# Group norm on one Trainium2 core: scale and offset of the packed blocks from a matrix product, and the inverse root's first guess read from PSUM

## The chip, the cores and the metric

The kernel runs on one core of one Trainium2 chip. The metric is the device time of one execution in microseconds (us), taken as the median of several executions. Beside these timed runs there is one profiled execution, whose hardware profile (the page and the trace) gives the durations, starts and waits of every instruction. Where the text gives a time such as "at 1079.81", it is counted from the start of that execution's span.

A core has five engines with queues of their own: PE (TensorE, matrix products; PEld is its loading of weights), DVE (VectorE), ACT (ScalarE), POOL (GpSimd) and SP (SyncE, which issues most DMAs here). SBUF is the on-chip memory of 128 partitions ("rows"), PSUM the small memory into which PE writes.

## What is computed

The input x has shape (16, 56, 56, 384): 16 images, 384 channels last, float32. Two residual layers follow each other, each of which works on a group norm (32 groups of 12 channels, statistics over a whole image):

```python
def _gn(v, G=32, eps=1e-5):
    g = v.reshape(B_, H_, W_, G, C_ // G)
    m = jnp.mean(g, axis=(1, 2, 4), keepdims=True)
    s = jnp.var(g, axis=(1, 2, 4), keepdims=True)
    return ((g - m) / jnp.sqrt(s + eps)).reshape(v.shape)
...
x = x + _L0_conv_ref(_gn(x), L0_conv_w_qkv, L0_conv_w_proj, L0_conv_b_proj)
x = x + _L1_conv_ref(_gn(x), L1_conv_w)
```

Layer 0 (`_L0_conv_ref`) is a dilated neighbourhood attention: a 384 to 1152 product gives q, k and v, 12 heads of 32 channels attend to 3x3 neighbours with dilation 1, 2 or 3 (four heads each), and a 384 to 384 product projects the result. Layer 1 (`_L1_conv_ref`) is a depthwise 3x3 convolution whose taps are the signs of `w`.

## The kernel before, in words

**Tiling.** An image is cut into 7 chunks of 8 image rows (PX = 448 pixels), so there are 112 chunks m = 7b + c. Work is done with channels on the partitions: three blocks of 128 channels (NG = 3).

**Stages of a chunk.** `plan_a` loads x, transposes it to channels-first (PE, pt_x, L478), takes statistics (`bn_stats`, L493) and stores it in DRAM (xd). `plan_b` loads it again, normalises it on ACT, makes q, k, v (products pq and pkv, L530, copied out by ACT: k at L543), multiplies q and k (DVE, t, L595), sums by head (PE, ps, L576), takes the softmax (transposes pt_s, L619), spreads the weights over the channels (PE, pb_a, L663), multiplies them with v (DVE, w, L674), sums over neighbours (POOL, L684, L687, L688) and projects (po, L701). `plan_c` does the convolution ten chunks later. Two of its three channel blocks use **packed blocks**: a tile z holds, for 4 sets q of 32 channels, the three vertical neighbours ky on 3 x 32 = 96 partitions, so that one product (pc, L825) does a column of taps. `normalise` (L792, on ACT; for the last set of the last image L788, on DVE) applies scale and offset to z and takes them from mrz, which must lie on the 96 partitions in z's layout. `column` (L815, ACT) starts pc from the middle taps with scalars that `column_scalars` (L727 to L737, POOL) makes. The third block is done by ACT's products m (L897) and POOL's sums (L907, L912, L915). Results are transposed back (PE, pt_o, L924), copied by ACT (osb, L930) and stored (out_dram, L933).

**Group norm** (`group_norm`, L349 to L419) runs 18 times. Each normal call holds two sets (L = 2): layer 1 of image b, and layer 0 of image b + 2; four calls hold only one. Sixteen of them include a layer 1 set (`for_convolution`). Its steps, each a piece between two `yield`s:

- DVE: `bn_aggr`, mean and variance of each channel over the chunks (ch).
- PE pm (L363): sums over the 12 channels of a group, three products with the selector gsel (128 rows x 32 columns); DVE L365 scales it into pair.
- PE pb (L370): the group's mean back on the channels with gselT (32 rows x 128 columns); DVE dev L373, POOL L375, L376: squared deviation plus channel variance.
- PE pv (L381): group sums of that. DVE L385 makes the variance plus eps (v); L388 and L389 make a first guess of 1/sqrt(v) by integer arithmetic on v's bits (shift right by one, then constant minus it).
- POOL L392 to L395, three times: Newton steps; L396: the offset. pair then holds offset and scale for 32 groups on 32 partitions.
- PE pp (L401): offset and scale on the channels; DVE L404 copies them to mr.
- SP: mr goes to DRAM as mrd (L409), and in the next piece three DMAs (L414) read it back in z's layout as mrz.

pm, pb, pv, pp, pt_x, pkv, po, pt_s and pt_o all take turns in two PSUM buffers (ps_mt).

**Order of the work.** Every piece has a due time, written out by hand in the table WHEN and counted in units of which a chunk has STEP = 9; a group norm of layer 1 of image b begins at STEP x (7b + 6) plus the offsets of WHEN["statistics"]. All pieces are sorted by time and issued in that order. Between FROM = 81 and UNTIL = 1022 units each engine's queue is pinned to the order in which pieces are issued (`pin`, for PE, DVE, ACT, POOL and SP). Before and after that, so in the first nine chunks of work and in the convolutions of the last image, a scheduler of the tile framework chooses the order by its own reckoning. At the start selectors are built by POOL from memsets and affine selections, in parallel with the weight loads. In the last image no attention stands beside the convolution any more, z is called z_last and xg is called xg_last there, and the third block's taps are done by DVE (`taps_last`, L888).

Of the kernel before, what the change touches and what calls it, by code (L numbers as in the profile page):

```python
# [8 lines left out]
F32 = mybir.dt.float32  # L9
BF16 = mybir.dt.bfloat16  # L10
I32 = mybir.dt.int32
AF = mybir.ActivationFunctionType
ALU = mybir.AluOpType
# [4 lines left out]
P = 128  # L18
HEADS = 4
HD = 32  # L20
NG = 3
NTAP = 9
NQ = 4
# [3 lines left out]
GN_CH = 12  # L27
GN_G = 32
# [3 lines left out]
RSQRT_BITS = 0x5F3759DF  # L32
# [9 lines left out]
    v=[[11.109, 11.185, 12.149], [14.632, 15.913, 18.706], [17.166, 18.74, 20.057]],  # L42
# [29 lines left out]
def dilated_attention_then_binary_conv(  # L72
# [28 lines left out]
    nc = tc.nc  # L101
    B, H, W, C = x.shape
    PX = ROWS * W
# [5 lines left out]
    K3 = 3 * HD  # L109
    JG = NG - 1  # L110

    def place(p):

        g, o = divmod(p, NTAP)
        return NG * o + g
# [4 lines left out]
    const = ctx.enter_context(tc.tile_pool(name="const", bufs=1))  # L120
    ps_mt = ctx.enter_context(tc.tile_pool(name="ps_mt", bufs=2, space=PSUM))
# [19 lines left out]
    for p in range(NPAD):  # L141

        v = place(p) if p < NG * NTAP else p
        nc.gpsimd.affine_select(
            out=perm[:, v, :], in_=perm[:, v, :], compare_op=ALU.not_equal, fill=1.0,
            base=-(32 * (p % 4) + 4 * (p // 4)), pattern=[[-1, HEADS]], channel_multiplier=1,
# [1 line left out]
    permf = perm.rearrange("p v h -> p (v h)")  # L148


    gsel = const.tile([P, NG, GN_G], F32, name="gsel")
    gselT = const.tile([GN_G, NG, P], F32, name="gselT")
    nc.gpsimd.memset(gsel, 1.0)
    nc.gpsimd.memset(gselT, 1.0)
    for j in range(NG):
        for lo, s in ((0, 1), (GN_CH - 1, -1)):
            nc.gpsimd.affine_select(
                out=gsel[:, j], in_=gsel[:, j], compare_op=ALU.is_ge, fill=0.0,
                base=s * P * j + lo, pattern=[[-s * GN_CH, GN_G]], channel_multiplier=s,
            )  # L160
            nc.gpsimd.affine_select(
                out=gselT[:, j], in_=gselT[:, j], compare_op=ALU.is_ge, fill=0.0,
                base=s * P * j + lo, pattern=[[s, P]], channel_multiplier=-s * GN_CH,
            )


    wqkvT = const.tile([P, NG, 3 * C], F32, name="wqkvT")
# [16 lines left out]
    st_p = ctx.enter_context(tc.tile_pool(name="st_p", bufs=2))  # L184
    dr_p = ctx.enter_context(tc.tile_pool(name="dr_p", bufs=3, space=DRAM))
# [4 lines left out]
    y_p = ctx.enter_context(tc.tile_pool(name="y_p", bufs=4))  # L190
# [3 lines left out]
    xg_p = ctx.enter_context(tc.tile_pool(name="xg_p", bufs=2))  # L194
    m_p = ctx.enter_context(tc.tile_pool(name="m_p", bufs=3))
    o_p = ctx.enter_context(tc.tile_pool(name="o_p", bufs=2))


    kv = []
# [149 lines left out]
    def group_norm(sets):  # L349

        L = len(sets)
        ch = st_p.tile([P, L, NG, 2], F32, tag=f"ch{L}", name="ch")
# [4 lines left out]
                        nc.vector.bn_aggr(ch[:, n, j, :], stats()[:, j].rearrange("p c s -> p (c s)"))  # L357
            yield

        pair = st_p.tile([GN_G, L, 3], F32, tag=f"pair{L}", name="pair")  # L360
        pm = ps_mt.tile([P, 512], F32, tag="mt", name="pm")
        for j in range(NG):
            nc.tensor.matmul(pm[:GN_G, 0:L], gsel[:, j], ch[:, :, j, 0], start=(j == 0), stop=(j == NG - 1))  # L363
        yield
        nc.vector.tensor_scalar_mul(pair[:, :, 2], pm[:GN_G, 0:L], -1.0 / GN_CH)  # L365
        yield

        pb = ps_mt.tile([P, 512], F32, tag="mt", name="pb")
# [3 lines left out]
        dev = st_p.tile([P, L, NG], F32, tag=f"dev{L}", name="dev")  # L372
# [5 lines left out]

        pv = ps_mt.tile([P, 512], F32, tag="mt", name="pv")
        for j in range(NG):  # L380
            nc.tensor.matmul(pv[:GN_G, 0:L], gsel[:, j], dev[:, :, j], start=(j == 0), stop=(j == NG - 1))  # L381
        yield
        var = st_p.tile([GN_G, 3, L], F32, tag=f"var{L}", name="var")
        v, r, t = var[:, 0], var[:, 1], var[:, 2]
        nc.vector.tensor_scalar(v, pv[:GN_G, 0:L], 1.0 / GN_CH, 1e-5, op0=ALU.mult, op1=ALU.add)  # L385

        ri = r.bitcast(I32)
        nc.vector.tensor_single_scalar(ri, v.bitcast(I32), 1, op=ALU.arith_shift_right)  # L388
        nc.vector.tensor_scalar(ri, ri, -1, RSQRT_BITS, op0=ALU.mult, op1=ALU.add)  # L389
        yield  # L390
        for step in range(3):
            nc.gpsimd.tensor_tensor(t, r, r, ALU.mult)  # L392
# [1 line left out]
            nc.gpsimd.tensor_scalar(t, t, -0.5, 1.5, op0=ALU.mult, op1=ALU.add)  # L394
            nc.gpsimd.tensor_tensor(pair[:, :, 1] if step == 2 else r, r, t, ALU.mult)  # L395
        nc.gpsimd.tensor_tensor(pair[:, :, 0], pair[:, :, 2], pair[:, :, 1], ALU.mult)  # L396
        yield

        pp = ps_mt.tile([P, 512], F32, tag="mt", name="pp")
        for j in range(NG):  # L400
            nc.tensor.matmul(pp[:, 2 * L * j : 2 * L * (j + 1)], gselT[:, j], pair[:, :, 0:2], start=True, stop=True)  # L401
        yield
        mr = st_p.tile([P, NG, L, 2], F32, tag=f"mr{L}", name="mr", bufs=5 - L)
        nc.vector.tensor_copy(mr.rearrange("p j l s -> p (j l s)"), pp[:, : 2 * L * NG])  # L404
        yield
        mrz = None
        if sets[0][2]:
            mrd = dr_p.tile([P, JG, 2], F32, tag="mrd", name="mrd")
            nc.sync.dma_start(mrd, mr[:, :JG, 0, :])  # L409
        yield  # L410
        if sets[0][2]:
            mrz = st_p.tile([K3, JG, NQ, 2], F32, tag="mrz", name="mrz")
            for ky in range(3):
                nc.sync.dma_start(  # L414
                    mrz[ky * HD : (ky + 1) * HD], mrd.rearrange("(q c) j s -> c j q s", c=HD)
                )
        yield
        for n, (_, done, for_convolution) in enumerate(sets):
            done(mr[:, :, n], mrz) if for_convolution else done(mr[:, :, n])  # L419
# [643 lines left out]
```

## Time and profile before

| what | value |
|---|---|
| median of 3 executions | 5050.63 us (5050.13 to 5052.91) |
| profiled execution | 5050.42 us |
| its span on the core | 5048.7 us, so 1.7 us lie around it |
| mean granted PE clock | 0.977 of full speed |
| busy: PE, DVE, POOL, ACT | 96%, 89%, 84%, 51% of the span |
| group norms: pm begins | 46.7, 237.2, then every 299 us or so from 479.2 to 4658, last 4904.3 |
| products of the group norm, records | pm 108, pb 108, pv 108, pp 108 |
| mrd<-mr, mrz<-mrd | 16 and 48 DMAs, 2 KB each, 6.9 and 2.9 us from issue to landing |

A page of the profile gives busy time and share of each engine, a chart in 40 slices, and the chain of work that ended last (followed back from the last instruction, at each step to what released it). Below these stand groups of instructions, `line engine operation out<-in (partitions x elements) xcount | busy, mean ns of one | idle time of the engine before them, and what ended most of it`. The view of one tile adds `min/median/max` in ns. In a timeline a line is `start us, length us, engine, line, operation`, with the engine's idle time before it in brackets. Float32 products appear as two records of weights and matmul each, so three products of the code are "x6".

### The profile page before, as it was taken

To read this page: it belongs to the slowest core of one execution; us is meant where nothing else is said; L and a number is where in the kernel's file an instruction comes from. 1 tells how busy PE (TensorE), PEld (TensorE's weight loads), DVE (VectorE), ACT (ScalarE), POOL (GpSimd) and SP (SyncE) were. 2 spreads that over 40 slices of the span, in tenths; PEclk is the share of its full clock that TensorE was granted. 3 is DMA by queue.
4 is the path that set the end of the run, shared out by engine and by line. 5 is a ranking of instruction groups with operands and counts; after the bars stand their busy time and mean duration, and the time that the engine had idled before them with its cause. 6 is when DMAs were issued, how large, how long until landed. Compare 5 with 4: busy or idle time off the path is not lost.

```text
span 5048.7 us, 69318 instructions
## 1 busy us (share of the span) xinstructions
PE 4833.2 (96%) x23433; PEld 2213.7 (44%) x23433; DVE 4513.4 (89%) x4710; ACT 2573.4 (51%) x4645; POOL 4226.0 (84%) x2894
## 2 busy tenths in 40 slices
PE   7999999999999999999999999999999999999954
PEld 4444444444444444444444444444444444444421
DVE  4888999999999999999999999999999999999846
ACT  3212555555555555555555555555555555555454
POOL 2677889988888888888889888888888888999970
PEclk9999999999999999999999999999999999999965
DMA  5434666666666666666666666666666666655554
GB/s 172 122 100 123 179 175 171 175 172 177 174 177 178 170 176 167 179 177 173 174 168 174 178 177 178 175 176 170 176 173 174 179 175 176 154 147 147 133 149 134
DMA packets 831097, 836.37 MB, mean 166 GB/s; under 512 B 379795, under 2 KB 800022, under 8 KB 830742
## 3 DMA queue, kind: packets, MB, share of 16 engines
q1 hardware_dynamic: 822758, 819.95, 60.3%
q10 hardware_dynamic: 7984, 12.00, 0.7%
q8 instruction: 185, 3.03, 0.3%
q14 instruction: 170, 1.39, 0.1%
HBM read 477.52 MB, written 231.24 MB: 140 GB/s over the span
## 4 chain that ended last, share of the span: by engine, by line
PE 81%; POOL 7%; DVE 3%; DMA 3%; issue 3%; ACT 2%; SPq 0%; ACTq 0%; POOLq 0%; DVEq 0%
PE pkv L530 26%; PE pq L530 14%; PE po L701 13%; PE ps L576 11%; PE pb_a L663 5%; PE pc L825 5%; POOL w L684 3%; PE pt_o L924 3%; PE pt_x L478 3%; DVE w L674 1%; DMA mrd<-mr 1%; POOL m L907 1%; DVE t L595 1%; PE pt_s L619 1%; DMA mrz<-mrd 1%
## 5 line engine op out<-in xcount | busy, mean ns | idle before, releaser
L684 POOL TENSOR_TENSOR w<-w 128x1344 f32<-128x1344 f32 x672 | 2052.5, 3054 | 164.4 <-DVE w L674 116.3
L674 DVE TENSOR_TENSOR w<-pb_a,v 128x1344 f32<-128x1344 f32 x1008 | 1563.4, 1551 | 206.8 <-PE pb_a L663 158.5
L530 PE MATMUL pkv<-xn,wqkvT 128*128 128x448 f32 x3924 | 1594.3, 546 | 0.0
L595 DVE TENSOR_TENSOR t<-pq,k 128x1344 f32<-128x1344 f32 x1008 | 1547.6, 1547 | 11.3 <-PE ps L576 6.5
L530 PEld LDWEIGHTS pkv<-xn,wqkvT 128*128 128x128 f32 x3924 | 718.5, 190 | 647.7 <-issue 644.4
L907 POOL TENSOR_TENSOR m<-m 128x1344 f32<-128x1344 f32 x210 | 641.2, 3053 | 290.3 <-ACT m L897 290.1
L701 PE MATMUL po<-y,wprojT 128*128 128x448 f32 x2016 | 822.7, 553 | 12.1 <-ACT osb L930 7.2
L530 PE MATMUL pq<-xn,wqkvT 128*128 128x448 f32 x1962 | 809.6, 548 | 0.1
L543 ACT COPY v<-pkv 128x448 f32<-128x448 f32 x336 | 180.1, 536 | 977.6 <-PE pt_o L924 487.5
L576 PE MATMUL ps<-t,sel 128*32 128x448 f32 x6048 | 660.5, 546 | 2.7 <-DVE t L595 2.0
L792 ACT ACTIVATE z<-z,mrz 96x448 f32<-96x448 f32 x840 | 569.8, 750 | 26.2 <-DMA mrz<-mrd 21.1
L897 ACT ACTIVATE m<-zg,ktap 128x448 f32<-128x448 f32 x945 | 550.3, 658 | 5.5 <-POOL m L907 4.8
L530 PEld LDWEIGHTS pq<-xn,wqkvT 128*128 128x128 f32 x1962 | 360.5, 190 | 397.0 <-issue 299.0
L701 PEld LDWEIGHTS po<-y,wprojT 128*128 128x128 f32 x2016 | 359.5, 191 | 346.7 <-issue 256.8
L663 PE MATMUL pb_a<-aT,spread 24*128 24x448 bf16 x3024 | 369.7, 360 | 55.6 <-DVE w L674 46.2
L930 ACT COPY osb<-pt_o 112x384 f32<-112x384 f32 x420 | 191.2, 480 | 432.3 <-PE pt_o L924 416.5
L687 POOL TENSOR_TENSOR y<-w 128x448 f32<-128x448 f32 x336 | 382.4, 1138 | 31.0 <-PE po L701 5.6
L843 DVE SCALAR_TENSOR_TENSOR pc<-x,cs,pc 128x440 f32<-128x440 f32 (+3 forms) x560 | 376.1, 673 | 31.7 <-issue 8.6
L688 POOL TENSOR_TENSOR y<-y,w 128x448 f32<-128x448 f32 x336 | 382.1, 1137 | 26.0
L663 PEld LDWEIGHTS <-spread 24*128 24x128 bf16 x3024 | 100.8, 91 | 480.9 <-issue 414.4
L576 PEld LDWEIGHTS ps<-t,sel 128*32 128x32 f32 x6048 | 169.5, 109 | 295.4 <-issue 285.5
L543 ACT COPY k<-pkv 128x448 f32<-128x448 f32 x336 | 179.3, 534 | 221.6 <-PE pkv L530 221.5
(141 smaller groups left out, 4638.0 us busy)
## 6 DMA issues: line engine op xcount, KB each, us to landing
z<-x1d SPq DMA_DIRECT2D x570, 224.0 KB, 4.3
xr<-xd SPq DMA_DIRECT2D x112, 672.0 KB, 5.8
x1d<-xr SPq DMA_DIRECT2D x112, 672.0 KB, 5.2
xn<-xd SPq DMA_DIRECT2D x109, 672.0 KB, 5.4
xin<-in_x_dram SPq DMA_DIRECT2D x105, 672.0 KB, 6.1
xd<-xa SPq DMA_DIRECT2D x315, 224.0 KB, 3.4
out_dram<-osb SPq DMA_DIRECT2D x420, 168.0 KB, 3.5
x<-x1d SPq DMA_DIRECT2D x80, 560.0 KB, 4.8
```

What stands on the lines that cost most here:

```text
L530: nc.tensor.matmul(dst[:, :PX], wqkvT[:, cc, o0 : o0 + P], had["xn"][:, cc, :], start=(cc == 0), stop=(cc == NG - 1))
L576: return nc.tensor.matmul(had["ps"][32 * j : 32 * j + 32, :PX], sel[:, s0 : s0 + 32], tk, start=(issued[j] == 1), stop=(issued[j] == len(r ...
L595: nc.vector.tensor_tensor(t.rearrange("p k (r w) -> p k r w", w=W), q3, k3, ALU.mult)
L663: return nc.tensor.matmul(pb[:, kx, :PX].rearrange("p (s n) -> p s n", s=NSUB), spread[rows_of, v % 2, :], had["a"][rows_of, :, v // 8, :] ...
L674: nc.vector.tensor_tensor(w.rearrange("p k (r w) -> p k r w", w=W), pb[:, :, :PX].rearrange("p k (r w) -> p k r w", w=W), three(kv[1][g][m ...
L684: nc.gpsimd.tensor_tensor(w0, w0, w, ALU.add)
L687: nc.gpsimd.tensor_tensor(y, w0[:, 0], w0[:, 1], ALU.add)
L688: nc.gpsimd.tensor_tensor(y, y, w0[:, 2], ALU.add)
L701: nc.tensor.matmul(po[:, :PX], wprojT[:, g, j * P : (j + 1) * P], had[f"y{g}"], start=(g == 0), stop=(g == NG - 1))
L792: nc.scalar.activation(z, z, AF.Identity, bias=mrz[:, j, q, 0:1], scale=mrz[:, j, q, 1:2])
L897: nc.scalar.activation(rows(t[:, kx]), zp[:, ky : ky + ROWS, kx : kx + W], AF.Copy, scale=ktap[:, JG, o : o + 1])
L907: nc.gpsimd.tensor_tensor(had["m"], had["m"], t, ALU.add)
```

## The change

Two things are changed in `group_norm`, and what they need is built at the start.

First, mrz isn't sent through DRAM any more. The selector gsel gets 64 columns per block of channels in place of 32: the 32 as before, and 32 that repeat selectors for the packed blocks (4 columns for each of the 8 = JG x NQ parts). pm and pv take two neighbouring blocks of it, 128 columns, as weights (`groups(j)`), of which the last 64 give rows that nothing uses. So pm and pv give 128 rows, and pair lies on 128 partitions. A mask `own` spreads offset and scale by part (POOL, `apart`, 128 x 16), and one more product with a constant matrix gselz puts them, in z's layout, into the same PSUM tile pp; DVE's one copy takes 28 columns in place of 12 to SBUF, of which mr and mrz are views. The 64 DMAs are gone; the three `yield`s stay, so the later pieces keep their due times.

Second, the first guess: DVE writes v twice, into PSUM and into SBUF (both from pv), and one `tensor_scalar` reads the PSUM copy as an integer, multiplies by −0.5, adds the constant, and writes the guess r into SBUF. Three DVE instructions stand in place of three.

At the start POOL also builds own, 32 small copies, and a tile `to_pack` (taken from the pool of y); PE multiplies its two parts into pz, and DVE copies the result to gselz.

```diff
--- before.py
+++ after.py
@@ -148,20 +148,29 @@
     permf = perm.rearrange("p v h -> p (v h)")
 
 
-    gsel = const.tile([P, NG, GN_G], F32, name="gsel")
-    gselT = const.tile([GN_G, NG, P], F32, name="gselT")
-    nc.gpsimd.memset(gsel, 1.0)
+    PARTS = JG * NQ
+    gsel = const.tile([P, NG + 1, 2 * GN_G], F32, name="gsel")
+    gselT = const.tile([P, NG, P], F32, name="gselT")
+    nc.gpsimd.memset(gsel, 0.0)
+    nc.gpsimd.memset(gsel[:, :NG, :GN_G], 1.0)
     nc.gpsimd.memset(gselT, 1.0)
     for j in range(NG):
         for lo, s in ((0, 1), (GN_CH - 1, -1)):
             nc.gpsimd.affine_select(
-                out=gsel[:, j], in_=gsel[:, j], compare_op=ALU.is_ge, fill=0.0,
+                out=gsel[:, j, :GN_G], in_=gsel[:, j, :GN_G], compare_op=ALU.is_ge, fill=0.0,
                 base=s * P * j + lo, pattern=[[-s * GN_CH, GN_G]], channel_multiplier=s,
             )
             nc.gpsimd.affine_select(
                 out=gselT[:, j], in_=gselT[:, j], compare_op=ALU.is_ge, fill=0.0,
                 base=s * P * j + lo, pattern=[[s, P]], channel_multiplier=-s * GN_CH,
             )
+    own = const.tile([P, PARTS], F32, name="own")
+    nc.gpsimd.memset(own, 1.0)
+    for lo, s in ((-GN_G, 1), (GN_G + 3, -1)):
+        nc.gpsimd.affine_select(
+            out=own, in_=own, compare_op=ALU.is_ge, fill=0.0, base=lo, pattern=[[-4 * s, PARTS]], channel_multiplier=s,
+        )
+    gselz = const.tile([P, P], F32, name="gselz")
 
 
     wqkvT = const.tile([P, NG, 3 * C], F32, name="wqkvT")
@@ -194,6 +203,28 @@
     xg_p = ctx.enter_context(tc.tile_pool(name="xg_p", bufs=2))
     m_p = ctx.enter_context(tc.tile_pool(name="m_p", bufs=3))
     o_p = ctx.enter_context(tc.tile_pool(name="o_p", bufs=2))
+
+    to_pack = y_p.tile([P, PX], F32, tag="y", name="to_pack")
+    packed = to_pack[:, : JG * P].rearrange("p (j g) -> p j g", j=JG)
+    fold = to_pack[:, JG * P : (JG + 1) * P].rearrange("p (a c) -> p a c", c=HD)
+    nc.gpsimd.memset(to_pack, 0.0)
+    for part in range(PARTS):
+        j, q = divmod(part, NQ)
+        g0, c0 = part * HD // GN_CH, GN_G + 4 * part
+        for g in range(NG):
+            nc.gpsimd.tensor_copy(gsel[:, g, c0 : c0 + 4], gsel[:, g, g0 : g0 + 4])
+        nc.gpsimd.tensor_copy(packed[q * HD : (q + 1) * HD, j, c0 : c0 + 4], gsel[q * HD : (q + 1) * HD, j, g0 : g0 + 4])
+    for q in range(P // HD):
+        nc.gpsimd.affine_select(
+            out=fold, in_=fold, compare_op=ALU.not_equal, fill=1.0, base=-q * HD,
+            pattern=[[0, P // HD], [-1, HD]], channel_multiplier=1,
+        )
+    pz = ps_mt.tile([P, 512], F32, tag="mt", name="pz")
+    for j in range(JG):
+        nc.tensor.matmul(
+            pz[:, :P], packed[:, j], fold.rearrange("p a c -> p (a c)"), start=(j == 0), stop=(j == JG - 1)
+        )
+    nc.vector.tensor_copy(gselz, pz[:, :P])
 
 
     kv = []
@@ -357,12 +388,15 @@
                         nc.vector.bn_aggr(ch[:, n, j, :], stats()[:, j].rearrange("p c s -> p (c s)"))
             yield
 
-        pair = st_p.tile([GN_G, L, 3], F32, tag=f"pair{L}", name="pair")
+        def groups(j):
+            return gsel[:, j : j + 2].rearrange("p a g -> p (a g)")
+
+        pair = st_p.tile([P, L, 3], F32, tag=f"pair{L}", name="pair")
         pm = ps_mt.tile([P, 512], F32, tag="mt", name="pm")
         for j in range(NG):
-            nc.tensor.matmul(pm[:GN_G, 0:L], gsel[:, j], ch[:, :, j, 0], start=(j == 0), stop=(j == NG - 1))
-        yield
-        nc.vector.tensor_scalar_mul(pair[:, :, 2], pm[:GN_G, 0:L], -1.0 / GN_CH)
+            nc.tensor.matmul(pm[:, 0:L], groups(j), ch[:, :, j, 0], start=(j == 0), stop=(j == NG - 1))
+        yield
+        nc.vector.tensor_scalar_mul(pair[:, :, 2], pm[:, 0:L], -1.0 / GN_CH)
         yield
 
         pb = ps_mt.tile([P, 512], F32, tag="mt", name="pb")
@@ -378,15 +412,15 @@
 
         pv = ps_mt.tile([P, 512], F32, tag="mt", name="pv")
         for j in range(NG):
-            nc.tensor.matmul(pv[:GN_G, 0:L], gsel[:, j], dev[:, :, j], start=(j == 0), stop=(j == NG - 1))
-        yield
-        var = st_p.tile([GN_G, 3, L], F32, tag=f"var{L}", name="var")
+            nc.tensor.matmul(pv[:, 0:L], groups(j), dev[:, :, j], start=(j == 0), stop=(j == NG - 1))
+        yield
+        var = st_p.tile([P, 3, L], F32, tag=f"var{L}", name="var")
         v, r, t = var[:, 0], var[:, 1], var[:, 2]
-        nc.vector.tensor_scalar(v, pv[:GN_G, 0:L], 1.0 / GN_CH, 1e-5, op0=ALU.mult, op1=ALU.add)
-
-        ri = r.bitcast(I32)
-        nc.vector.tensor_single_scalar(ri, v.bitcast(I32), 1, op=ALU.arith_shift_right)
-        nc.vector.tensor_scalar(ri, ri, -1, RSQRT_BITS, op0=ALU.mult, op1=ALU.add)
+        for to in (pv[:, L : 2 * L], v):
+            nc.vector.tensor_scalar(to, pv[:, 0:L], 1.0 / GN_CH, 1e-5, op0=ALU.mult, op1=ALU.add)
+        nc.vector.tensor_scalar(
+            r.bitcast(I32), pv[:, L : 2 * L].bitcast(I32), -0.5, float(RSQRT_BITS), op0=ALU.mult, op1=ALU.add
+        )
         yield
         for step in range(3):
             nc.gpsimd.tensor_tensor(t, r, r, ALU.mult)
@@ -394,26 +428,29 @@
             nc.gpsimd.tensor_scalar(t, t, -0.5, 1.5, op0=ALU.mult, op1=ALU.add)
             nc.gpsimd.tensor_tensor(pair[:, :, 1] if step == 2 else r, r, t, ALU.mult)
         nc.gpsimd.tensor_tensor(pair[:, :, 0], pair[:, :, 2], pair[:, :, 1], ALU.mult)
+        if sets[0][2]:
+            apart = st_p.tile([P, PARTS, 2], F32, tag="apart", name="apart")
+            nc.gpsimd.tensor_tensor(
+                apart, pair[:, 0, 0:2].unsqueeze(1).to_broadcast([P, PARTS, 2]),
+                own.unsqueeze(2).to_broadcast([P, PARTS, 2]), ALU.mult,
+            )
         yield
 
         pp = ps_mt.tile([P, 512], F32, tag="mt", name="pp")
         for j in range(NG):
             nc.tensor.matmul(pp[:, 2 * L * j : 2 * L * (j + 1)], gselT[:, j], pair[:, :, 0:2], start=True, stop=True)
-        yield
-        mr = st_p.tile([P, NG, L, 2], F32, tag=f"mr{L}", name="mr", bufs=5 - L)
-        nc.vector.tensor_copy(mr.rearrange("p j l s -> p (j l s)"), pp[:, : 2 * L * NG])
-        yield
-        mrz = None
-        if sets[0][2]:
-            mrd = dr_p.tile([P, JG, 2], F32, tag="mrd", name="mrd")
-            nc.sync.dma_start(mrd, mr[:, :JG, 0, :])
-        yield
-        if sets[0][2]:
-            mrz = st_p.tile([K3, JG, NQ, 2], F32, tag="mrz", name="mrz")
-            for ky in range(3):
-                nc.sync.dma_start(
-                    mrz[ky * HD : (ky + 1) * HD], mrd.rearrange("(q c) j s -> c j q s", c=HD)
-                )
+        n_mr, n_z = 2 * L * NG, 2 * PARTS if sets[0][2] else 0
+        if n_z:
+            nc.tensor.matmul(
+                pp[:, n_mr : n_mr + n_z], gselz, apart.rearrange("p a s -> p (a s)"), start=True, stop=True
+            )
+        yield
+        both = st_p.tile([P, n_mr + n_z], F32, tag=f"mr{n_z}_{L}", name="mr", bufs=5 - L)
+        nc.vector.tensor_copy(both, pp[:, : n_mr + n_z])
+        mr = both[:, :n_mr].rearrange("p (j l s) -> p j l s", j=NG, l=L)
+        mrz = both[:K3, n_mr:].rearrange("p (j q s) -> p j q s", j=JG, q=NQ) if n_z else None
+        yield
+        yield
         yield
         for n, (_, done, for_convolution) in enumerate(sets):
             done(mr[:, :, n], mrz) if for_convolution else done(mr[:, :, n])
```

## The prediction

> **What bounds the kernel now.** I read the page first, then the chain of waits and each engine's timeline around the group norms, because everything the change touches happens once an image.
>
> ```profile
> PE 4833.2 (96%) x23433; PEld 2213.7 (44%) x23433; DVE 4513.4 (89%) x4710; ACT 2573.4 (51%) x4645; POOL 4226.0 (84%) x2894
> PE 81%; POOL 7%; DVE 3%; DMA 3%; issue 3%; ACT 2%; SPq 0%; ACTq 0%; POOLq 0%; DVEq 0%
> ...
> L792 ACT ACTIVATE z<-z,mrz 96x448 f32<-96x448 f32 x840 | 569.8, 750 | 26.2 <-DMA mrz<-mrd 21.1
> ```
>
> TensorE is the bound: 96% busy. The start of the one tile pt_s per chunk gives the cadence: an ordinary chunk takes 41.95 to 41.97 us and PE is never idle in it. So PE idle time that goes is gained in full, and PE time that is added is paid in full. The chunk in which a group norm's statistics run takes 45.75 us (+3.80) and the next one 42.9 to 44.0. The chain of waits through one such pair (image boundary at 1075 to 1110 us) tells why:
>
> ```profile
> 1079.63 0.16 DVE var L385
> ...
> 1079.81 2.32 DVE var L388
> ...
> 1082.24 1.57 DVE w L674
> ...
> 1083.85 0.37 PE pb_a L663 x3
> ...
> 1093.51 0.18 DVE mr L404
> ...
> 1093.71 6.88 DMA mrd<-mr
> ...
> 1102.01 2.16 DMA mrz<-mrd
> ...
> 1104.32 0.13 ACT z L792
> ...
> 1108.82 0.47 ACT k L543
> ...
> 1109.34 0.60 PE pt_x L478 x4
> ```
>
> Two stalls. **Stall 1** is L388, an integer shift of 32x2 elements. POOL's timeline, and PE's with its idle time in brackets, explain it:
>
> ```profile
> 1079.06 3.04 POOL L684 TENSOR_TENSOR w<-w 128x1344 f32<-128x1344 f32 x1
> ```
> ```profile
> 1083.85 0.37 PE L663 MATMUL pb_a<-aT,spread 24*128 24x448 bf16 x3 [1.38 <-DVE w L674]
> ```
>
> L388 starts at 1079.81 and ends at 1082.12, just after POOL's 3.04 us multiplication (1082.10). Its 18 executions take 131/2296/2390 ns (min/median/max), and 131 to 140 ns where POOL has nothing to do. The multiplication w of L674 queued behind it on DVE is late, and PE waits for w's buffer before pb_a. At 12 boundaries PE's idle time there is 1.35 to 1.46 us, 1.29 at 489 and 1.27 at 4374, none at 4658. **Stall 2** is the DRAM round trip: mr is copied at 1093.5, mrz is there at 1104.2. ACT's normalisation of z waits for it, ACT's copy k behind that is late, and PE's pt_x waits for k's bank: 0.71 us of idle just there, 0.72 in that chunk.
>
> **What the Trainium skill says.** "SBUF — State Buffer", section "Who interferes with whom": VectorE and GpSimd share one port pair, an exclusive lock; a `tensor_scalar` in a 2-port mode fully blocks until the GpSimd instruction ends, one with at most one SBUF input outside these modes doesn't contend. "VectorE: DVE Perf Modes", section "What auto-detection actually checks", puts an instruction in that mode if its single source and its destination are both in SBUF with even or equal outermost dimensions. The trace agrees: L388 (SBUF to SBUF) takes 2.3 us, while L365 and L385, which read PSUM and write as few elements to SBUF, take 135 to 149 ns in every one of 36 executions, L385 at 1079.63 under the same POOL multiplication. "TensorE: Matmul & The Clock Gate", section "LDWEIGHTS (loading the stationary operand)": the load's time goes by the columns, not the rows. The trace agrees: 113 ns for 128*32 (pm), 187 ns for 32*128 (pb). "DMA: Bandwidth & Descriptors", section "Anatomy of one DMA — SWDGE (gpsimd) path", gives a fixed cost of about 2 us, mostly the receipt. Here 2 KB take 6.9 (mrd) and 2.9 us (mrz), on SP's queue.
>
> **Part 1: first guess from PSUM.** Removed: L388 and L389. Added: a second scaling of pv (L385's kind, 0.15, into PSUM) and one `tensor_scalar` that reads it from PSUM and writes r in SBUF. The number of DVE instructions stays three, all with a PSUM source, so by the 36 executions above each should take 0.15 us whatever POOL does. Then w starts at about 1080.3 instead of 1082.24 and is done before PE asks for it at 1082.47. What is late next there? PE's next pt_o is at 1081.93 and takes a buffer of the ring in which pv lies; pv is now read until 1080.2, so 1.7 us are spare. Gain: the whole stall, 12 x 1.45 (the difference in PE's shift against an ordinary chunk, which is 0.07 above the idle shown) + 1.29 + 1.27 = **20.0 us**.
>
> **Part 2: mrz from one more product.** Removed: one mrd and three mrz DMAs per convolution group norm, 64 in all. SP's queue moves too: the x load (L473), 6.5 us into the chunk after a boundary because it stood behind these issues, goes out at about 1.5 as in other chunks; it landed before it was needed, so that is worth nothing by itself. mrz will be ready with mr, about 10 us earlier than now, and z's normalisation starts at 6.9 us into the chunk as in ordinary ones instead of 8.2 to 9.3. Ordinary chunks with as many ACT products ahead of k have no stall, so nothing is late next. PE's shift at pt_x in the 12 chunks is .98 .88 1.71 1.23 1.36 1.05 1.69 1.05 1.52 1.95 1.38 1.68 = 16.5, and 0.79 at 4400: gain **17.3 us**. POOL gets one small multiplication (0.27 us with its dependence, like the root's other steps); POOL then waits 1.9 us for ACT before L907, which hides it. If that cover were missing it would cost at most 15 x 0.27 = 4. The other POOL steps go from 32 to 128 rows at the same elements per row, no cost. DVE's copy L404 goes from 12 to 28 columns, below 0.03 us.
>
> **Part 3: wider products, on PE and so paid.** pm and pv become 128*128. The trace has no such product with so few columns; the nearest rows are pb and pp:
>
> ```profile
> L363 PEld LDWEIGHTS pm<-ch,gsel x108: 106/113/158, 46.7 to 4904.5; 128*32 128x32 f32 x108
> L363 PE MATMUL pm<-ch,gsel x108: 163/171/213, 46.7 to 4904.6; 128*32 128x2 f32 x84, 128*32 128x1 f32 x24
> ```
> ```profile
> L370 PEld LDWEIGHTS pb<-pair,gselT x108: 181/187/333, 47.6 to 4906.0; 32*128 32x128 f32 x108
> L370 PE MATMUL pb<-pair,gselT x108: 245/246/368, 47.6 to 4906.1; 32*128 32x2 f32 x84, 32*128 32x1 f32 x24
> ```
>
> On the chain, six records of pm take 0.28 us and six of pb 0.76. So pm and pv each cost +0.48, and gselz's product, two records at 0.127, +0.25: 1.21 a boundary, x 15 = **+18.2 us**. Bounds: if the rows count and not the columns, pm and pv cost nothing and only 0.25 stays (+3.8); if they cost what six of pb took under the lower clock of the end (1.45 at 4904.99, that is 0.24 each), 2.8 each boundary (+42). I take pb's price of the middle.
>
> **Part 4: start.** POOL builds the selectors first: 32 small copies (eight parts, four each) and some twenty masks. At some 0.16 us for each of POOL's small steps, as in cs at 4915.72 to 4916.57, these and the memsets come to about 13 us, so that pz, PE's first product, comes at about 19 us where pt_x came at 7.15. Before the change PE waited at 23.6 to 30.80 for ACT, which stood behind a load's queue, so three chunks of transposes (8 us) fit into 20 to 31. I take +2, between 0 and +8 if POOL's copies take twice as long, and +0.5 for the second group norm, in which nothing is hidden.
>
> **Part 5: end.** The last image has no work of attention beside it. mr is ready at 4915.5, but mrz was issued only at 4929.0 to 4930.4, because SP was held by two output stores; the last image's first convolution ran at 4939.6 to 4942. After: mr at about 4917.7 (the wide products at the slow clock cost 2.2), no DMA, z normalised by 4924, and POOL's xg (4925.7 to 4927.1) gates what PE does first; so the first convolution comes at 4930, 9.5 us earlier. Later chunks of that image take 16.5 us each in a chain of loads, products and stores that mrz isn't in, but taps that were done ahead in that gap are then late. I take −6.5; from −12 to +3.
>
> **Sum.** −20.0 − 17.3 + 18.2 + 2.5 − 6.5 = −23.1. Profiled execution 5050.4 (span 5048.7 and 1.7 around it), so 5027.3; the median of the runs is 5050.63, 0.2 above it, which I leave out.
>
> **Rivals.** (A) *One of the two stalls stays*: the new first guess writes SBUF and might take the lock all the same, or another transfer holds z. Loss of 20 or 17: about 5046. For it: DVE shares with a POOL that is 84% busy. Against: L365 and L385 do just that without waiting. (B) *Another wait takes a place*: after mrz, z or k waits for something 0.6 us later at each of 13 boundaries (8 us) and the start costs 5 more: 5040. Against: ordinary chunks of the same form show no idle at all. (C) *The end keeps its cadence* and gains nothing: 5033.8. For it: the 16.5 us per chunk there. (D) *Slower, by the wide products alone*: at 0.24 each, as at the end, they cost 42, more than the 37.3 that both stalls give; with 6 at the start and nothing at the end it gives 5061. It decides from 37.3/15 = 2.5 us a boundary. Against: PE's clock is 0.9 or more in all middle slices and the six pb took 0.76 there.
>
> **How the numbers follow.** Forecast as summed 0.53, C 0.20, B 0.12, A 0.10, D 0.05. 0.2%, 10.1 us, is about what a measurement of this kernel can tell from no change: below 5040.5 is faster, above 5060.7 slower. Forecast and C are faster, B half so: 0.79; A and half of B 0.16; D 0.05. The forecast's own range takes the unknowns together (wide products −10 to +5, start −2.5 to +6, end −5.5 to +9.5): 5013 to 5040. To leave out no more than 2 in 10 it reaches to A's 5046.
>
> **What will show it.** L388 gone and no successor above 0.2 us; no idle before pb_a; boundary chunk at about 45.5 (−1.45 + 1.21), the next at 42.0 with no idle before pt_x; six of pm and pv at 0.76; PE's first product at about 19 us; first convolution of the last image near 4930, counted on the clock of before. I am wrong if the new first guess still takes 2 us (A), if boundary chunks are longer than 46.3 (D), or if a new idle appears ahead of pt_x (B).

## The result

The kernel after takes 5018.03 us (median of 4 executions, 5015.8 to 5018.41) beside 5051.77 us for the kernel before in the same runs (4, 5050.13 to 5057.05): ratio 0.9931, 95% interval 0.9913 to 0.9948. In later runs it took 5011.26 us beside 5043.83 us, ratio 0.9937 (0.9924 to 0.9949). The profiled execution took 5018.26 us, its span 5015.4 us: 33.3 us less than the span before, where the prediction had 23.1. Below, a chunk is counted from one start of pt_s to the next, and a boundary chunk is one in which a group norm runs.

The page of the kernel after, with busy time, the chain by engine, and the normalisation of z:

```profile
PE 4840.0 (97%) x23469; PEld 2230.2 (44%) x23469; DVE 4483.8 (89%) x4711; ACT 2571.0 (51%) x4645; POOL 4239.8 (85%) x2951
PE 83%; POOL 7%; issue 2%; DVE 2%; ACT 1%; DMA 0%; SPq 0%; ACTq 0%; POOLq 0%; DVEq 0%
...
L829 ACT ACTIVATE z<-z,mr 96x448 f32<-96x448 f32 x840 | 569.7, 750 | 7.3 <-DMA z<-x1d 7.3
```

PE is busy 6.8 us longer than before and the span is shorter: what went was idle time. The chain's 3% of DMA is gone, and ACT's 21.1 us of waiting for mrz with it.

The DVE timeline of the kernel after at the same boundary (start, length, instruction, idle before it) and POOL's:

```profile
1075.38 0.17 DVE L420 TENSOR_SCALAR pv<-pv 128x2 f32<-128x2 f32 x1 [0.95 <-PE pv L415]
1075.59 0.16 DVE L420 TENSOR_SCALAR var<-pv 128x2 f32<-128x2 f32 x1
1075.66 0.15 DVE L421 TENSOR_SCALAR var<-pv 128x2 int32<-128x2 int32 x1
1076.14 1.56 DVE L711 TENSOR_TENSOR w<-pb_a,v 128x1344 f32<-128x1344 f32 x1 [0.33 <-PE pb_a L700]
```
```profile
1074.42 3.05 POOL L721 TENSOR_TENSOR w<-w 128x1344 f32<-128x1344 f32 x1
```

The three small instructions run under POOL's multiplication (1074.42 to 1077.47) in 0.17, 0.16 and 0.15 us, where the shift had taken 2.31. w no longer waits for DVE; it waits for PE, and PE's pb_a has no idle time ahead of it:

```profile
1077.86 0.27 PE L961 MATMUL pt_o<-ident,xg 128*112 128x128 f32 x1
1078.07 0.36 PE L700 MATMUL pb_a<-aT,spread 24*128 24x448 bf16 x3
```

In the next chunk ACT's normalisation of z starts when ACT is free, with no bracket behind it (ACT's timeline), and so does pt_x (PE's):

```profile
1097.61 2.72 ACT L829 ACTIVATE z<-z,mr 96x448 f32<-96x448 f32 x4
```
```profile
1103.01 0.55 PE L515 MATMUL pt_x<-ident,xin 112*128 112x112 f32 x4
```

The cadence says where the time went. The table sets the change of the interval from pt_s to pt_s, summed over the chunks of a kind, beside the terms of the prediction:

| stretch | predicted | measured |
|---|---|---|
| start, to the chunk at 458 us | +2.5 | −2.5 |
| 14 boundary chunks with the shift's stall (45.75 to 44.95 us at most of them) | −3.1 (−20.0 + 14 x 1.21) | −11.2 |
| 13 chunks after a boundary (42.9–45.3 to 41.95) | −17.3 | −19.6 |
| boundary at 4636 us, no stall before | +1.2 | +0.7 |
| other chunks to 4806 us | 0 | +1.6 |
| the rest, with the last image | −6.5 | −2.2 |
| sum | −23.2 | −33.2 |

### The profile page after: what moved, and what is told of

Read it like the earlier page. It is cut to its first block, busy times and chain, and to the rows that moved or that the text cites. A ratio compares the mean times of both kernels' runs of the same rounds, so it can differ in the third digit from the quotient of the medians.

```text
span 5015.4 us, 69405 instructions
## 1 busy us (share of the span) xinstructions
PE 4840.0 (97%) x23469; PEld 2230.2 (44%) x23469; DVE 4483.8 (89%) x4711; ACT 2571.0 (51%) x4645; POOL 4239.8 (85%) x2951
## 4 chain that ended last, share of the span: by engine, by line
PE 83%; POOL 7%; issue 2%; DVE 2%; ACT 1%; DMA 0%; SPq 0%; ACTq 0%; POOLq 0%; DVEq 0%
PE pkv L567 27%; PE po L738 14%; PE pq L567 13%; PE ps L613 11%; PE pb_a L700 5%; PE pc L862 5%; PE pt_o L961 3%; POOL w L721 3%; PE pt_x L515 2%; PE pt_s L656 1%; POOL m L944 1%; DVE w L711 1%; DVE t L632 1%; POOL y L724 1%; POOL y L725 1%
## 5 line engine op out<-in xcount | busy, mean ns | idle before, releaser
L829 ACT ACTIVATE z<-z,mr 96x448 f32<-96x448 f32 x840 | 569.7, 750 | 7.3 <-DMA z<-x1d 7.3
```

What stands on the lines that cost most here:

```text
L829: nc.scalar.activation(z, z, AF.Identity, bias=mrz[:, j, q, 0:1], scale=mrz[:, j, q, 1:2])
```

## The experiments

### One half at a time

First guess alone, on the kernel before:

```diff
-        nc.vector.tensor_scalar(v, pv[:GN_G, 0:L], 1.0 / GN_CH, 1e-5, ...)
-        nc.vector.tensor_single_scalar(ri, v.bitcast(I32), 1, op=ALU.arith_shift_right)
-        nc.vector.tensor_scalar(ri, ri, -1, RSQRT_BITS, op0=ALU.mult, op1=ALU.add)
+        for to in (pv[:GN_G, L : 2 * L], v):
+            nc.vector.tensor_scalar(to, pv[:GN_G, 0:L], 1.0 / GN_CH, 1e-5, ...)
+        nc.vector.tensor_scalar(r.bitcast(I32), pv[:GN_G, L : 2 * L].bitcast(I32), -0.5, float(RSQRT_BITS), ...)
```

> The kernel before with the first guess alone changed (read from PSUM); mrz still goes through DRAM and the products stay narrow. Theory (the shift from SBUF to SBUF waited for POOL's lock on the shared port): three DVE instructions of 0.15 us each, no idle before pb_a, boundary chunks 45.75 - 1.45 = 44.3 us, the chunk after a boundary still 42.9 to 44.0; 12 x 1.45 + 1.29 + 1.27 = 20 us less than before, about 5031 us. Rival (the gain of the change came from the DRAM path, the shift's stall only moved somewhere else): boundary chunks stay above 45 us and the time is above 5040 us.

Measured: 5020.03 us, ratio 0.9951 (0.9939 to 0.9964); the kernel before took 5044.05 beside it, so 24.0 us less. Boundary chunks are 44.35 us (−1.40), with no idle before pb_a; the chunks after them still wait for mrz:

```profile
1095.41 2.73 ACT L792 ACTIVATE z<-z,mrz 96x448 f32<-96x448 f32 x4 [1.48 <-DMA mrz<-mrd]
```
```profile
1100.45 0.60 PE L478 MATMUL pt_x<-ident,xin 112*128 112x112 f32 x4 [1.06 <-ACT k L543]
```

The boundary chunks give 19.5 us in all, the 20 of the theory. Where the rest of the 24.0 came from is less sure: the start is 4.9 us shorter than in the profile of before, but that one is from the first runs, in which the kernel before took 5050 us.

The other half: the kernel after with the old first guess, on 128 rows.

```diff
-        for to in (pv[:, L : 2 * L], v):
-            ...
+        nc.vector.tensor_scalar(v, pv[:, 0:L], 1.0 / GN_CH, 1e-5, op0=ALU.mult, op1=ALU.add)
+        nc.vector.tensor_single_scalar(ri, v.bitcast(I32), 1, op=ALU.arith_shift_right)
+        nc.vector.tensor_scalar(ri, ri, -1, RSQRT_BITS, op0=ALU.mult, op1=ALU.add)
```

> The kernel after with the old first guess (shift, then constant minus it, both SBUF to SBUF, now on 128 rows); mrz comes from the product. Theory (the two stalls add up): the shift takes 2.3 us again, pb_a waits 1.4 us, boundary chunks 44.95 + 1.45 = 46.4 us, the next chunk 41.95 with no wait for mrz; 20 us above the kernel after, about 5038 us. Rival (the stalls overlap, one alone gives most of the gain): below 5028 us.

Measured: 5034.25 us, ratio 0.9982 (0.9976 to 0.9989), 9.8 us below before. The product of the two ratios is 0.9933, the kernel after's 0.9931: within the intervals the halves add up, and the rival of overlapping stalls falls. Boundary chunks are 46.1 us, and the chunks after them 41.95, the same to 0.02 us as in the kernel after. DVE's and PE's timelines show the stall back, a little smaller than the 1.38 of before:

```profile
1082.02 1.88 DVE L422 TENSOR_SCALAR var<-var 128x2 int32<-128x2 int32 x1
```
```profile
1085.62 0.37 PE L700 MATMUL pb_a<-aT,spread 24*128 24x448 bf16 x3 [1.05 <-DVE w L711]
```

I had expected 46.4. The wide products delay DVE's start of the shift, but not the end of POOL's multiplication for which it waits, so part of their cost vanishes in the stall. The experiments on width below show this alone.

### What made the shift wait

The kernel before with the two integer steps done for one element per row at a time:

```diff
-        nc.vector.tensor_single_scalar(ri, v.bitcast(I32), 1, op=ALU.arith_shift_right)
-        nc.vector.tensor_scalar(ri, ri, -1, RSQRT_BITS, op0=ALU.mult, op1=ALU.add)
+        for l in range(L):
+            nc.vector.tensor_single_scalar(ri[:, l : l + 1], vi[:, l : l + 1], 1, op=ALU.arith_shift_right)
+            nc.vector.tensor_scalar(ri[:, l : l + 1], ri[:, l : l + 1], -1, RSQRT_BITS, ...)
```

> The kernel before with the shift and the constant minus it done for one element per row at a time: four instructions of 32x1 from SBUF to SBUF where there were two of 32x2. Theory (only an instruction in a 2-port mode waits, and one element per row is not in one, as the shift of 32x1 took 0.14 us at 4664.6 beside POOL's multiplication): each 0.14 us, 20 us less than before, about 5031 us. Rival (every DVE instruction from SBUF to SBUF waits for a running POOL instruction): the first of the four takes 2.3 us and nothing is gained, about 5050 us.

Measured: 5024.57 us, 19.5 us less than before, ratio 0.9965 (0.9951 to 0.9978), boundary chunks 44.31 us. The tile's view (duration min/median/max in ns) of this kernel:

```profile
L389 DVE TENSOR_SCALAR var<-var x32: 129/140/142, 48.9 to 4882.2; 32x1 int32<-32x1 int32 x32
L390 DVE TENSOR_SCALAR var<-var x32: 130/141/142, 49.1 to 4882.4; 32x1 int32<-32x1 int32 x32
```

None of 64 instructions from SBUF to SBUF waited, though POOL's multiplication was running at the start of 30 of the 32 shifts. The kernel before with only the shift reading PSUM:

```diff
-        nc.vector.tensor_single_scalar(ri, v.bitcast(I32), 1, op=ALU.arith_shift_right)
+        nc.vector.tensor_single_scalar(ri, pv[:GN_G, L : 2 * L].bitcast(I32), 1, op=ALU.arith_shift_right)
         nc.vector.tensor_scalar(ri, ri, -1, RSQRT_BITS, op0=ALU.mult, op1=ALU.add)
```

> The kernel before with the variance also written to PSUM and the shift reading it there; the second step of the guess, constant minus it, stays SBUF to SBUF with 32x2 elements. Theory (the lock): the shift takes 0.15 us and the second step now waits in its place for POOL's multiplication, some 2 us; pb_a waits 1.3 us or a little more as before; 5051 us within 3. Rival (the shift as an integer operation is slow, or only the first step after the variance waits): no instruction above 0.2 us, 20 us less, about 5031 us.

Measured: 5041.69 us beside 5044.05, ratio 0.9997 (0.9989 to 1.0005), boundary chunks 45.54 us. The same view:

```profile
L389 DVE TENSOR_SCALAR var<-pv x18: 135/136/138, 48.8 to 4896.8; 32x2 int32<-32x2 int32 x14, 32x1 int32<-32x1 int32 x4
L390 DVE TENSOR_SCALAR var<-var x18: 131/2053/2152, 49.0 to 4896.9; 32x2 int32<-32x2 int32 x14, 32x1 int32<-32x1 int32 x4
```

The wait went over to the next instruction that has source and destination in SBUF and two elements per row. So it is neither the shift, nor integers, nor "SBUF to SBUF" as such. In the kernel before all 14 shifts of 32x2 ended 0.01 to 0.02 us after POOL's multiplication, whether they took 1.3 us or 2.4. That is what a lock of the 2-port mode would do, and the conditions that the Trainium skill gives in "VectorE: DVE Perf Modes", section "What auto-detection actually checks", are in line with all of these kernels. No run has an odd count above one, so what the even count does by itself is not shown; and every instruction that waited was an integer one.

### The price of width

pm and pv alone made wide, on the kernel before (columns of zeros):

```diff
+    gsel_w = const.tile([P, NG, P], F32, name="gsel")
+    gsel = gsel_w[:, :, :GN_G]
-            nc.tensor.matmul(pm[:GN_G, 0:L], gsel[:, j], ch[:, :, j, 0], ...)
+            nc.tensor.matmul(pm[:, 0:L], gsel_w[:, j], ch[:, :, j, 0], ...)
...
+            nc.tensor.matmul(pv[:, 0:L], gsel_w[:, j], dev[:, :, j], ...)
```

> The kernel before with pm and pv alone made 128 columns wide (zeros in the added columns; only the first 32 rows of their results are used). The price of width by itself. Theory A (a load goes by its columns, at the price that pb had): +0.48 us each, boundary chunks 45.75 + 0.96 = 46.7 us, about 14 us above before. Theory B (what costs is the step from a product of one shape to one of another, 32 and 128 columns or rows, which before and after differ in): pm and pv +0.4 and +0.2 as in the kernel after, boundary chunks 46.3 to 46.4 us, and pb and pp unchanged; about 9 us above before.

Measured: 5045.46 us beside 5044.62, ratio 1.0001 (0.9993 to 1.001), boundary chunks 45.74 us: nothing, which neither theory had. PE's idle time before pb_a shrank from 1.38 to 0.78 us:

```profile
1083.08 0.37 PE L665 MATMUL pb_a<-aT,spread 24*128 24x448 bf16 x3 [0.78 <-DVE w L676]
```

and the shift at this boundary took 1.62 us in place of 2.31. So the width does cost PE 0.6 us, and all of it lay in the stall. At 4636 us, the boundary where the kernel before has no stall, the chunk was 0.6 us longer (44.11 against 43.53): there it was paid. The price itself is read from how much later the next instruction on PE starts than in the ordinary chunk before (in us):

| kernel | pm | pb | pv | pp, with gselz's product where there is one |
|---|---|---|---|---|
| before: pm, pv 128\*32; pb, pp 32\*128 | 0.31 | 0.84 | 0.49 | 0.56 |
| wide only: pm, pv 128\*128 | 0.72 | 0.82 | 0.69 | |
| after: all 128\*128 | 0.71 | 0.56 | 0.68 | 0.92 |
| 64 columns: pm, pv 128\*64; pb, pp 64\*128 | 0.46 | 0.85 | 0.63 | 0.99 |
| 64 columns, pair on 128 rows: pb, pp 128\*128 | 0.46 | 0.59 | 0.65 | 1.07 |

pb and pp alone on 128 rows, on the kernel before (pair is one of four tiles cleared once):

```diff
-    gselT = const.tile([GN_G, NG, P], F32, name="gselT")
+    gselT = const.tile([P, NG, P], F32, name="gselT")
...
-            nc.tensor.matmul(pb[:, j * L : (j + 1) * L], gselT[:, j], pair[:, :, 2], ...)
+            nc.tensor.matmul(pb[:, j * L : (j + 1) * L], gselT[:, j], pair_w[:, :, 2], ...)
```

> The kernel before with gselT and pair on 128 rows (zeros in the added ones, the pairs in four tiles that are cleared once), so that pb and pp are 128*128 products and pm and pv stay narrow. Theory A (the load goes by columns alone): no change of boundary chunks, 45.75 us. Theory B (products of 32 rows cost more on PE than those of 128, as pb's 0.84 us before and 0.56 us after suggest): boundary chunks shorter by 0.2 to 0.5 us, 3 to 7 us less in all.

Measured: 5044.77 us beside 5044.62, ratio 1.0002 (0.9994 to 1.0011), boundary chunks 45.86 us, 0.1 longer. pm and pb together took 0.89 us where they had taken 1.15, so pb got 0.26 shorter; but PE then waited 0.13 us for pv's operand, and the idle time before pb_a grew to 1.46. Again the stall hid it, here a gain. pp, which comes behind the stall, got 0.13 longer on 128 rows (0.69 against 0.56), which is about the 0.1. Both experiments missed for the same reason: while DVE waits for POOL, PE's work ahead of it is free in both directions.

That pb gains from 128 rows and pp loses has a trace. At the boundary at 1075 us, the weight loads (PEld) and products of pb, first in the kernel before, then on 128 rows:

```profile
1076.04 0.74 PEld L370 LDWEIGHTS pb<-pair,gselT 32*128 32x128 f32 x6 [0.65 <-DVE pair L365]
1076.04 0.82 PE L370 MATMUL pb<-pair,gselT 32*128 32x2 f32 x6
```
```profile
1075.86 0.19 PEld L377 LDWEIGHTS pb<-pair,gselT 128*128 128x128 f32 x1 [0.19 <-DVE pair L372]
1076.23 0.73 PE L377 MATMUL pb<-pair,gselT 128*128 128x2 f32 x6
```

With 32 rows the first load starts together with its product, when the 128-row product ahead of it is over; with 128 rows it starts 0.37 us before its product, while the one ahead still runs. The operand isn't the reason: pair was ready at 1075.51 in the kernel before. Medians over 12 boundaries say the same for the other kernels of this section: with 32 or 64 rows pb's first load starts 0.47 us after the start of the product ahead, with 128 rows at that start. Before pp stands pb_a, of 24 rows, and there it is the other way: a load of 32 rows starts together with pb_a's last product, one of 64 or 128 rows 0.29 us later. So for these two the price goes with the change of rows from one product to the next, not with few rows; why the load isn't started earlier is not shown.

The kernel after, cut to the 64 columns and rows that are used:

```diff
-            return gsel[:, j : j + 2].rearrange("p a g -> p (a g)")
+            return gsel[:, j]
...
-        pair = st_p.tile([P, L, 3], F32, tag=f"pair{L}", name="pair")
+        pair = st_p.tile([2 * GN_G, L, 3], F32, tag=f"pair{L}", name="pair")
```

> The kernel after with pm and pv on the 64 columns that are used instead of 128, and pair, pb, pp and gselz's product on 64 rows. Theory A (columns set the price): pm and pv at about 0.2 us less each than after, boundary chunks 44.95 - 0.3 = 44.6 us, 4 to 5 us less than after. Theory B (128*128 is the form that goes best between other products of that form): no gain or a loss, boundary chunks 44.9 to 45.3 us, 0 to 5 us more than after.

Measured: 5014.94 us beside 5044.62, ratio 0.9941 (0.9929 to 0.9954); boundary chunks 45.06 us, 0.11 longer than after. pm came down by 0.25 us and pb went up by 0.29 (table), so theory A fails: the columns set pm's price, but 64 rows cost pb what 32 had cost. The time is 3 us less than the 5018.03 of the kernel after, which is from the first runs; so both were run together, with a third:

> The kernel after unchanged, on the chip and in the call of the two that follow, to compare with. About 26 to 34 us below before.

> The 64-column kernel again, beside the kernel after. Its boundary chunks were 0.11 us longer than after's, its start 1.6 us and its end 2.4 us shorter. If these last two come from how the scheduler orders start and end, they repeat: 2 to 4 us below the kernel after; if they were chance, 1.5 us above it.

The third takes the 64 columns and sets pair on 128 rows:

```diff
-            nc.tensor.matmul(pb[:, j * L : (j + 1) * L], gselT[: 2 * GN_G, j], pair[:, :, 2], ...)
+            nc.tensor.matmul(pb[:, j * L : (j + 1) * L], gselT[:, j], pair_w[:, :, 2], ...)
```

> The 64-column kernel with pair on 128 rows (the added 64 are zeros, four tiles cleared once), so that pb and pp are 128*128 products and pm and pv 64 columns wide. Theory (a product of fewer than 128 rows costs pb 0.28 us more, and columns cost pm 0.25 us): boundary chunks 45.06 - 0.28 = 44.75 us, the shortest of all with mrz from the product, 3 to 4 us below the 64-column kernel. Rival (each form costs by its neighbours, and the sum is the same): 44.95 us or more.

Measured, beside 5043.83 for before: after 5011.26 (0.9937, 0.9924 to 0.9949), 64 columns 5012.66 (0.9940, 0.9927 to 0.9952), 64 columns with 128 rows 5012.80 (0.9938, 0.9925 to 0.9952). These are the same time. Of the 64 columns' two gains the shorter end repeated (136.2 us from the last pm to PE's last product, against 138.6), the shorter start didn't. The boundary chunk of the third is 44.90 us, the shortest with mrz from a product, by 0.05 against after and not by the 0.2 expected: pb gave its 0.26, the last group of products took some of it back. None beats the kernel after by what can be measured.

### Start and end

The kernel before with a late start of PE:

```diff
+    late = y_p.tile([P, PX], F32, tag="y", name="late")
+    for _ in range(9):
+        nc.gpsimd.memset(late, 0.0)
+    pz = ps_mt.tile([P, 512], F32, tag="mt", name="pz")
+    nc.tensor.matmul(pz[:, :P], late[:, :P], late[:, P : 2 * P], start=True, stop=True)
+    nc.vector.tensor_copy(late[:, :P], pz[:, :P])
```

> The kernel before with nine clears of a 128x448 tile on POOL at the start and one product of PE that needs the last of them and stands ahead of the first transposes, as pz does after; the statistics are untouched. The start of PE moves from 7.2 to some 18 us. Theory (PE waits later for ACT and the input loads in any case, to 30 us): the first pt_s stays at 103 us within 1, no cost. Rival (the late start is paid): the first pt_s at 108 us or later, 5 to 10 us above before.

Measured: 5049.14 us beside 5043.83, ratio 1.001 (1.0004 to 1.0017). PE's timeline:

```profile
16.75 0.80 PE L203 MATMUL pz<-late 128*128 128x128 f32 x2 [16.75 <-POOL late L201]
17.34 0.95 PE L485 MATMUL pt_x<-ident,xin 112*128 112x112 f32 x4
25.76 1.75 PE L485 MATMUL pt_x<-ident,xin 112*128 112x112 f32 x8 [7.47 <-DVE late L204]
```

The first pt_s came 1.7 us late, although this start was worse than planned (the copy of pz held a PSUM buffer to 25.7). That is nearer to the theory's 1 than to the rival's 5, but the time, 5.3 us longer, is what the rival had. Where the other 3.6 us come from the profiled execution doesn't show, its span (5047.8 us) being 0.9 us below that of before, which is from the first runs. The run decides for neither.

The kernel after with the last stores issued by POOL:

```diff
-            queue = nc.sync if b < B - 1 else nc.scalar
+            queue = nc.sync if m < N - NCH - 4 else nc.gpsimd
```

> The kernel after with the output stores of the last eleven chunks issued by POOL, which has little to do there, in place of SP and ACT. It tests where the rest of the gain at the end went. Theory (SP stood for 11.8 us behind a store that waited for ACT, and the last image's loads of z behind it came late): the third convolution of the last image loses its wait of 7.0 us for z_last, and the end comes 3 to 5 us earlier than in the kernel after, about 5014 us. Rival (the end is set by its chain of about 17 us a chunk, through loads, ACT and DVE, whoever issues the stores): within 2 us of the kernel after.

Measured: 5023.60 us beside 5044.62, ratio 0.9959 (0.9946 to 0.9971), worse than after. Counted from the last pm, the convolutions of the last image (24 product records each) and the end of PE's last product came at the following times. The kernels end 3.7 to 3.8 us after that, the one with stores on POOL 6.0.

| kernel | first | second | third | fourth | end of PE |
|---|---|---|---|---|---|
| before | 35.4 | 45.3 | 62.0 | 76.1 | 140.6 |
| first guess only | 35.4 | 45.3 | 61.7 | 75.7 | 140.3 |
| mrz from the product only | 26.4 | 38.1 | 56.2 | 72.1 | 137.8 |
| after | 28.9 | 38.7 | 57.7 | 73.5 | 138.0 |
| after, stores on POOL | 34.9 and 42.0 (8 and 16 records) | 54.8 | 70.5 | 87.3 | 149.7 |

PE's 7.0 us wait for z_last was gone, but every convolution was later, the first by 6 us and the next three by 13 to 16, and PE's end by 12. The edit also made the scheduler order the end anew (each half of the first convolution now waited 5.4 us for ACT's pc), so it isn't a clean test, and neither the theory nor its rival is confirmed.

## Why the prediction was right, and where its sum was off

**Part 1, the first guess: right in mechanism and size.** 19.5 us in the boundary chunks of the kernel with this half alone, against 20.0. The four forms of the guess show what waits and for what: an instruction from SBUF to SBUF with two elements per row, for POOL's multiplication to end. A PSUM source is one way of several out of it. That a shared port is behind it no trace shows; it is the account that the prediction took from the Trainium skill, and every form fits it.

**Part 2, mrz: right in mechanism, its size from one execution.** 13 chunks gave 19.6 us against 17.3. 1.7 of the difference is one chunk (at 2591 us) that in the profile of before was 3.4 us longer than in the kernel after, where the prediction had counted 1.69. But 17.3 and 19.6 are both read from that one profile, so their nearness is partly luck. In the profiles of the six other kernels with mrz through DRAM, all from later runs, the same 13 chunks cost only 12.9 to 16.4 us over the 41.95 (41.29 in the last) that they take without it, and mrd<-mr took 4.6 to 6.6 us in place of 6.9. Nothing took the place of the wait. Rivals A and B are thereby out: no stall stayed and no new one came.

**Part 3, the wider products: the term that was mis-sized.** "So pm and pv each cost +0.48, and gselz's product, two records at 0.127, +0.25: 1.21 a boundary." Measured on boundary chunks, after against the first guess alone: 44.95 − 44.35 = 0.60. Two things failed in that step. I took record lengths from the chain (0.28, 0.76) where the start of the next instruction tells the price: pm rose by 0.40, pv by 0.19. And I left out that the wider pair also turns pb and pp from 32\*128 to 128\*128: pb, which I had taken as fixed, fell by 0.28. With +0.36 for pp and gselz's product that makes 0.67, near the 0.60. The term is 8.5 us too large over 14 boundaries, most of the 10 by which the sum was off. The tile's view of the kernel after shows what a reader of durations sees, and it misleads: per record pb got longer, 251 against 246 ns.

```profile
L404 PE MATMUL pb<-pair,gselT x108: 167/251/373, 46.4 to 4876.5; 128*128 128x2 f32 x84, 128*128 128x1 f32 x24
```

The gain lies not in pb's own records but in when its first weight load starts, 0.37 us ahead of its product. Rival D, slower by width, is refuted by the same number: it needed 2.5 us a boundary.

**Part 4, the start: right on the cover, wrong on the second group norm.** PE's first product came at 17.9 us, and the work that had waited until 30.8 us began at 30.1; the first pt_s was 0.6 us earlier. The second group norm, for which I added 0.5, got 2.2 us cheaper (two chunks together): the scheduler, which orders this part, let POOL do the root's steps ahead of a multiplication; before, pp had waited 3.75 us for them. No trace of before can tell such a reordering. In the repeated run of the kernel after, the stretch from the start to the chunk at 458 us (in the kernel before) gave 6.2 us instead of 2.5, and in the kernel with the first guess alone 4.9, so it is a term with a few us of its own spread.

**Part 5, the end: the right place, too large.** The first convolution of the last image came at 4902.6, not near 4930 minus the lead of about 31, that is 4899: 6.5 us earlier against the last pm and not 9.5. Then it was given back as the prediction feared, only more: 6.6 us ahead at the second convolution, 4.3 at the third, 2.6 at the fourth and at the end. PE's timeline has the place:

```profile
4931.35 4.72 PE L862 MATMUL pc<-z_last,kdiag 96*32 96x440 f32 x24 [7.04 <-DMA z_last<-x1d]
```

That z_last was late is shown for this execution; that SP's stores made it so was argued, and the run on it couldn't decide it. In the repeated run of the same kernel PE waited 6.04 us in this place for ACT's pc, behind the load of x, and the end came at 138.6: what is late there is not always z_last. The kernel with mrz from the product alone has the same end as after, 137.8 us from the last pm, and that with the first guess alone 140.3: the gain at the end belongs to the product. Rival C, no gain at the end, was nearer than my 6.5, though not right.

**The sum.** The terms' errors, −8 at the boundaries, −5 at the start, −2.3 in the chunks after them, +4.3 at the end and +1.6 in ordinary chunks, go the same way for the most part; 23 forecast, 33 found.

## What to carry to other kernels

A small VectorE instruction beside a long GpSimd one is worth a look at its operands: from SBUF to SBUF with two elements per row it stood here until the GpSimd instruction ended, and a PSUM source, or one element per row, freed it. Costs of edits on an engine don't add where a stall lies behind them: the width of the products was free as long as DVE waited for POOL, and cost 0.6 us when it no longer did. A stall that ends with a DMA should be sized from more than one execution. The price of a short product is read from the start of what follows it, in a chunk with and one without, not from its own record.

## What the runs showed that I had not expected

- In pb's place, between products of 128 rows, six product records of 64\*128 or 32\*128 held PE for 0.82 to 0.85 us, six of 128\*128 for 0.56 to 0.59, with loads of 187 to 192 ns and products of 246 to 251 ns in all of them. In pp's place, behind a product of 24 rows, six of 32\*128 took 0.56 and six of 128\*128 0.69. The Trainium skill, "TensorE: Matmul & The Clock Gate", section "LDWEIGHTS (loading the stationary operand)", has the load go by columns alone. The load records agree; what the product costs PE depends on its neighbours' rows as well.
- DVE's shift of 32x1 elements took 0.13 and 0.14 us under POOL's multiplication at 249 and 4664.6 us in the kernel before, the same instruction with 32x2 2.3 us. This stood in the trace of before and I had not used it in the prediction.
- Chunks after a boundary varied from 41.95 to 45.93 us from boundary to boundary, and at the same boundary from kernel to kernel (at 3490 us 43.96 in the kernel before, 45.93 in the one with pb and pp on 128 rows and 41.95 in the one with pm and pv wide), wherever mrz went through DRAM; they were 41.94 to 41.98 us at the same 12 boundaries in the profile of every kernel without it.
